# Queries and keys of eight-wide heads: projected dense and spread through DRAM, with two output tiles handled together

## The chip, the cores and the metric

The kernel runs on one core of one Trainium2 chip. The metric is the device time of one execution in microseconds, lower is better. A profiled execution also gives a span, from the first to the last instruction that the profile shows. The engines are PE (TensorE, matrix multiplication), DVE (VectorE), ACT (ScalarE), POOL (GpSimd) and SP (SyncE, which here issues every DMA). PEld is the loading of PE's stationary operand. Each engine takes its own instructions in the order in which they stand, and semaphores tie the engines together.

## The reference, cut to what matters

A model of four blocks works on x of 8 sequences x 256 tokens x 128 features. Each block adds a gated cross attention to a context of the same shape, and then a gated ffn. All of it is float32.

```
x += tanh(g_xattn[0]) * performer(layernorm(x), ctx)       # 16 heads of 8, 32 random features
x += tanh(g_ffn[0])   * (attn0(h) + moe0(h))               # h = layernorm(x); attn0: 16 heads of 8
x += tanh(g_xattn[1]) * topk_attn(layernorm(x), ctx)       # 8 heads of 64, best 64 of 256 keys
x += tanh(g_ffn[1])   * moe1(layernorm(x))
x += tanh(g_xattn[2]) * attn2(layernorm(x), ctx)           # 16 heads of 8
x += tanh(g_ffn[2])   * moe2(layernorm(x))                 # 8 experts and a shared one, 512 wide
x += tanh(g_xattn[3]) * topk_attn3(layernorm(x), ctx)      # 16 heads of 8, best 32 of 256 keys
x += tanh(g_ffn[3])   * moe_attn(layernorm(x))             # 16 experts
```

What the change touches is the attention with 16 heads of 8, in the ffn of block 0 and in the cross attentions of blocks 2 and 3:

```
q = (x @ Wq + bq) / sqrt(8);  k = ctx @ Wk + bk;  v = ctx @ Wv + bv      # split into 16 heads of 8
w = softmax(q @ k.T)            # block 3: over the best 32 keys of each row
out = (w @ v) @ Wo + bo         # block 0's ffn: no Wo, k and v from x itself
```

## The kernel before

The tokens stand in four groups of 512 (two sequences of 256 each), with x in the tiles `xs[g]` of [128 tokens, 4, 128]. Two streams of work are woven together by generators (`side_by_side`). One, `largest_scores`, runs the two top-k attentions: block 1's over all groups, then block 3's over all groups. The other, `others`, runs the rest in a list written out by hand: x0 (the performer), f0 (block 0's ffn), f1, x2, f2 and f3 for each of the four groups. A group of the first stream starts only when the second has finished what comes before it, and the other way round (`may_start`, `started`, `middle`, `largest_1`, `largest_3`). `T_START` holds the times by which the weaving paces the first stream. The generators give the order in which instructions are recorded; a scheduler with a timeline model of its own then sets the order on each engine.

A matmul over heads of 8 reads queries and keys as rows of 32 in the partitions: PE works on four strips of 32 rows at once, so each head has a strip in which eight rows are its data and the rest are zero. Row 8 carries a one in the keys (added by way of the bias, from the column `aug`), and the negated row maximum in the queries, so the shift of the softmax comes out of the same matmul. A tile of queries (`qT`, or `qTk` in block 3) is [128, 4, 256]: four chunks of four heads, for the 256 tokens of one sequence. To get it, `pad_heads` (L231) spreads the weights to 512 columns with zeros between the heads, and `heads_T` (L292) makes four matmuls of 128x256 (L299), one for each chunk, and four ACT passes that add the bias and scale (L305). Block 1's heads of 64 go through `heads_T` too, without a bias (L301).

`attention_T` serves block 0's ffn and block 2. Its `ready` makes the operands of one sequence, computes the scores once for the row maxima (`sm`, L687) and adds the maxima to the queries (L709); `weigh` computes the transposed scores (`sw`, L723), takes the exponential (L737) and multiplies by the values (L357). `attention_largest` serves blocks 1 and 3: `fetch` computes scores (`sp`, L420) into one of several rooms, block 3's selection takes the best 32 by MAX8 and MATCH_REPLACE8 on DVE (L385, L389), POOL makes the mask (L392), and PE adds it to the transposed scores (L574, L584). `prepare` of a sequence runs ahead where the first stream's sequence is known.

`heads_back` (L336) turns the products back to token rows, one tile of 128 tokens at a time: four transposes (L341), a reciprocal (L345) and a product (L347) into `o_sb`. Then it calls `done` for this tile: `out_proj` (L320) transposes (L324), copies (L326), multiplies by Wo (L330) and the bias row (L333), and `add_gated` (L288, L290) adds the result to x.

Every load goes through one helper, `load` (L123), on SP's queue; so all DMAs have line 124. Tiles come from pools with a fixed number of buffers: `work` has four of [128, 1024], `bank` four of PSUM and `qT`, `kT`, `qTk`, `kTk` two each. The three `we2` buffers hold the expert weights of block 2's ffn, which SP loads as buffers come free. `load_context` (L1318) loads and transposes the weights of blocks 2 and 3 through `work` tiles; block 3's `wq` and `wk` use the space of block 1's `wq1` and `wo1`.

At the start, POOL makes constants, multiplies the random features into a block-diagonal weight (L911) once sixteen small DMAs of the features (`rf`) have landed, spreads block 0's weights, and reduces a maximum over the partitions (L894) that the first exponentials of the keys wait for.

After the program that is timed stands a second, exact one, which runs only if a count of wrongly chosen keys is not zero.

Of the kernel before, what the change touches and what calls it, by code (L numbers as in the profile page):

```python
# [90 lines left out]
def gated_blocks_kernel(ctx: ExitStack, tc: tile.TileContext, a, out):  # L91
# [7 lines left out]
    psum = ctx.enter_context(tc.tile_pool(name="psum", bufs=2, space=PSUM))  # L99

    def program(exact):
# [21 lines left out]
        def load(dst, src):  # L123
            nc.sync.dma_start(out=dst, in_=src)
# [106 lines left out]
        def pad_heads(t, w):  # L231

            t = t.rearrange("p (h d) -> p h d", d=32)
            nc.gpsimd.memset(t, 0.0)
            nc.gpsimd.tensor_copy(t[:, :, 0:8], w.rearrange("p (h d) -> p h d", d=8))

        def padded_bias(src, name, scale=1.0):

            t = wt([P, 4], name)
            nc.gpsimd.memset(t, 0.0)  # L240
            for r in range(4):
                load(t[32 * r : 32 * r + 8, :], src.rearrange("(c r d) -> r d c", r=4, d=8)[r])
            if scale != 1.0:
                nc.vector.tensor_scalar_mul(t, t, scale)
            return t

# [41 lines left out]
        def add_gated(g, t, src, gate):  # L288

            nc.vector.scalar_tensor_tensor(xs[g][:, t, :], src, gate, xs[g][:, t, :], ALU.mult, ALU.add)  # L290
# [16 lines left out]

        def values16(w, srcT, width, tag):
# [11 lines left out]
        def out_proj(g, t, o_sb, chunks, w, bias, gate):  # L320

            pt = bank("pt_o")
            for c in range(chunks):
                nc.tensor.transpose(pt[:, c * P : (c + 1) * P], o_sb[:, c * P : (c + 1) * P], ident)  # L324
            oT = out2("oT")
            nc.scalar.copy(oT[:, 0 : chunks * P], pt[:, 0 : chunks * P])  # L326
            yield
            po = bank("po")
            for c in range(chunks):
                nc.tensor.matmul(  # L330
                    po[:, 0:D], lhsT=oT[:, c * P : (c + 1) * P], rhs=w[:, c, :], start=(c == 0), stop=False
                )
            nc.tensor.matmul(po[:, 0:D], lhsT=bias, rhs=biases, start=False, stop=True)  # L333
            add_gated(g, t, po[:, 0:D], gate)

        def heads_back(g, bb, oTs, done):  # L336

            for qc in range(2):
                pn = bank("pn").rearrange("p (c r d) -> p c r d", c=4, r=4)
                for c in range(4):  # L340
# [5 lines left out]
                o_sb = out2("o_sb")[:, 0:D].rearrange("p (c r d) -> p c r d", c=4, r=4)  # L346
                nc.vector.tensor_tensor(  # L347
                    o_sb, pn[:, :, :, 0:8], rec.unsqueeze(3).to_broadcast([P, 4, 4, 8]), ALU.mult
                )
                yield  # L350
                yield from done(g, 2 * bb + qc, o_sb.rearrange("p c r d -> p (c r d)"))
# [699 lines left out]
        wq0, wk0 = w0[:, 1024:1536], w0[:, 1536:2048]  # L1051
# [9 lines left out]
        pad_heads(wq0, st[:, 0:128])  # L1061
        pad_heads(wk0, st[:, 128:256])
        nc.gpsimd.tensor_copy(wv0, st[:, 256:384])
        bq0 = padded_bias(bqkv0[0:128], "bq0", INV_SQRT8)
        bk0 = padded_bias(bqkv0[128:256], "bk0")
        nc.vector.tensor_tensor(bk0, bk0, aug.to_broadcast([P, 4]), ALU.add)
# [12 lines left out]
        class block0_ffn:  # L1079
            def __init__(self, g):  # L1080
                def done(g, t, o):
                    add_gated(g, t, o, tgf[:, 0:1])
                    yield

                self.g, self.att = g, attention_T(g, self.operands, done)
# [19 lines left out]
            def operands(self, bb):  # L1105
                xnT = self.xnT[:, bb * S : (bb + 1) * S]
                qT = heads_T(wq0, xnT, bq0, INV_SQRT8, "qT")
                yield
                kT = heads_T(wk0, xnT, bk0, 1.0, "kT")
# [208 lines left out]
        def load_context(n, tq, tk):  # L1318
            pre = f"L{n}_xattn"
            wq = wt([P, 512], f"wq{n}", tq)  # L1320
            pad_heads(wq, transposed(a[f"{pre}_Wq"]))
            wk = wt([P, 512], f"wk{n}", tk)
            pad_heads(wk, transposed(a[f"{pre}_Wk"]))
# [564 lines left out]
```

## Time and profile before

| | |
|---|---|
| time, three runs | 2543.44, 2546.03, 2556.37 us; median 2546.03 |
| profiled execution: its time, its span | 2546.42 us, 2544.7 us |
| busy | PE 83%, DVE 69%, ACT 45%, POOL 35% of the span |
| mean granted clock of PE | 0.862 |
| DMA | 32.97 MB, 13 GB/s in the mean; from DRAM 29.53 MB read, 1.05 MB written |
| instructions in the profile | 35734 |

How to read it: busy time says how much of the span an engine worked, not how near it is to its limit. "The chain that ended last" is followed back from the last instruction, at each step to what released it; its shares say where a shorter step would have moved the end, until another chain takes over. A group's row gives the line, the engine, the operation, its tiles and shapes, the count, the busy time of the group and the mean of one in ns, and then how long the engine was idle just before and what ended that. A float32 matmul of this kernel leaves two matmul records, so a count on PE is twice the number of instructions. In the table of stages each column is an engine's busy time in that stretch, followed by the granted clock, the share of the DMA engines' time and the rate.

### The profile page before, as it was taken

Reading aid. Unit: us, or ns where it says so; the run is one execution under the profiler, and the core shown is the slowest. Engines: PE = TensorE matmul, PEld = TensorE weight load, DVE = VectorE, ACT = ScalarE, POOL = GpSimd, SP = SyncE. Lnnn points to the kernel's source line nnn. Section 1 sums busy time; section 2 is a strip of 40 time slices with the busy share of each in tenths; the row PEclk is TensorE's granted clock in tenths of the full one; section 3 lists DMA queues with packets and bytes.
Section 4 is the critical chain, followed back from the end, with each engine's and each line's share of the span. In section 5 each row is a group of like instructions: output and inputs, shape, how many; then the busy total and the mean of one; then the engine's idle time right before and its main releaser. Section 6 shows DMA issues by size and latency. Waiting matters only on the chain.

```text
span 2544.7 us, 35734 instructions
## 1 busy us (share of the span) xinstructions
PE 2123.7 (83%) x12068; PEld 1292.4 (51%) x12094; DVE 1762.5 (69%) x5463; ACT 1149.0 (45%) x2437; POOL 879.8 (35%) x2252
## 2 busy tenths in 40 slices
PE   7998888887878778888989868899676975988898
PEld 5655455554445444445444435445343444666677
DVE  4635757756765667665899879894798869798332
ACT  2236556546554677864355433464333542322101
POOL 3104434434432464531334324341233334233000
PEclk8999889978988889998599966899775986999999
DMA  2000001000000000010001100021000110000000
GB/s 63 6 1 2 1 1 32 1 1 1 1 1 1 1 26 1 26 34 22 1 1 42 34 1 1 1 59 50 1 1 1 42 42 1 1 5 1 5 5 6
DMA packets 47896, 32.97 MB, mean 13 GB/s; under 512 B 4747, under 2 KB 42838, under 8 KB 47702
## 3 DMA queue, kind: packets, MB, share of 16 engines
q1 hardware_dynamic: 47702, 30.58, 4.2%
q8 instruction: 97, 1.59, 0.3%
q14 instruction: 97, 0.79, 0.1%
HBM read 29.53 MB, written 1.05 MB: 12 GB/s over the span
## 4 chain that ended last, share of the span: by engine, by line
DVE 39%; PE 36%; ACT 13%; POOL 8%; issue 4%; DMA 0%; DVEq 0%; SPq 0%; ACTq 0%; POOLq 0%
DVE m L385 13%; DVE wk L389 12%; ACT signs L495 4%; PE sm L687 3%; PE sw L723 3%; PE ph L1476 3%; PE pp L299 3%; PE y L1445 2%; DVE nmz L695 2%; PE po L1635 2%; ACT sign L495 2%; PE oT L357 2%; PE o L1216 2%; DVE xe L851 2%; DVE list L542 1%
## 5 line engine op out<-in xcount | busy, mean ns | idle before, releaser
L392 POOL TENSOR_SCALAR mask<-rooms,m 128x256 bf16<-128x256 f32 x192 | 223.3, 1163 | 385.5 <-DVE m L385 353.4
L385 DVE MAX8 m<-wk 128x8 f32<-128x256 f32 x768 | 326.8, 426 | 37.0 <-DVE wk L389 0.9
L723 PE MATMUL sw<-qT,kT 32*128 32x256 f32 x1024 | 172.4, 476 | 68.3 <-ACT eK L599 24.1
L695 DVE TENSOR_REDUCE nmz<-sm 128x4 f32<-128x1024 f32 x128 | 154.9, 1219 | 105.1 <-PE sm L687 96.6
L389 DVE MATCH_REPLACE8 wk<-m,wk 128x256 f32<-128x256 f32 x512 | 208.9, 408 | 0.0
L495 ACT ACTIVATE signs<-room,nt 128x256 bf16<-128x256 f32 x288 | 145.9, 507 | 128.7 <-POOL nt L527 78.5
L687 PE MATMUL sm<-kT,qT 32*128 32x256 f32 x1024 | 152.6, 440 | 40.0 <-DVE nmz L695 28.4
L592 ACT ACTIVATE kept<-mask 128x1024 bf16<-128x1024 bf16 x64 | 67.6, 1057 | 227.3 <-POOL mask L392 227.1
L1476 PE MATMUL ph<-xnT,we 128*128 128x512 f32 x288 | 156.2, 638 | 15.5 <-ACT hT L1477 7.4
L723 PEld LDWEIGHTS sw<-qT,kT 32*128 32x128 f32 x1024 | 101.0, 222 | 128.4 <-DVE nmz L695 32.3
L737 ACT ACTIVATE eT<-sw 128x1024 f32<-128x1024 f32 x128 | 129.6, 1019 | 79.9 <-PE sw L723 73.9
L574 PE MATMUL sw<-qTk,kTk 32*128 32x256 f32 (+1 forms) x768 | 120.8, 456 | 53.6 <-DVE qTk L1383 35.2
L1445 PE MATMUL y<-hT,we 128*128 128x512 f32 x288 | 146.0, 620 | 0.6 <-DVE wb_sb L1457 0.6
L687 PEld LDWEIGHTS sm<-kT,qT 32*128 32x128 f32 x1024 | 92.3, 205 | 101.0 <-DVE nmz L695 42.9
L1477 ACT ACTIVATE hT<-ph,b 128x512 f32<-128x512 f32 x144 | 98.4, 686 | 98.8 <-PE ph L1476 94.4
L599 ACT ACTIVATE eK<-sw 128x1024 f32<-128x1024 f32 x96 | 96.6, 1019 | 89.4 <-PE sw L584 88.5
L420 PE MATMUL sp<-kTk,qTk 32*128 32x256 f32 (+1 forms) x768 | 121.1, 448 | 14.8 <-ACT eT L737 6.5
L357 PE MATMUL oT<-eT,va 128*32 128x256 f32 x1024 | 120.6, 449 | 10.2 <-ACT eT L737 9.3
L392 POOL TENSOR_SCALAR mask<-room,m 128x256 bf16<-128x256 f32 x64 | 74.5, 1164 | 155.2 <-DVE m L385 152.8
L574 PEld LDWEIGHTS sw<-qTk,kTk 32*128 32x128 f32 (+1 forms) x768 | 71.5, 212 | 96.1 <-issue 42.4
L420 PEld LDWEIGHTS sp<-kTk,qTk 32*128 32x128 f32 (+1 forms) x768 | 72.5, 209 | 59.5 <-issue 17.0
L387 POOL TENSOR_SCALAR nmk<-m 128x1 f32<-128x1 f32 x256 | 59.5, 232 | 100.7 <-DVE m L385 100.6
(381 smaller groups left out, 4976.2 us busy)
## 6 DMA issues: line engine op xcount, KB each, us to landing
we<-in_L_ffn_exp_w_dram SPq DMA_DIRECT2D x64, 256.0 KB
we<-in_L_ffn_shared_w_dram SPq DMA_DIRECT2D x8, 256.0 KB
x<-in_x_dram SPq DMA_DIRECT2D x4, 256.0 KB
big_ctx<-in_ctx_dram SPq DMA_DIRECT2D x4, 256.0 KB
w1f<-in_L_ffn_fc_w_dram SPq DMA_DIRECT2D x1, 1024.0 KB
w3a<-in_L_ffn_q_proj_dram SPq DMA_DIRECT2D x4, 256.0 KB
w3a<-in_L_ffn_k_proj_dram SPq DMA_DIRECT2D x4, 256.0 KB
w3b<-in_L_ffn_v_proj_dram SPq DMA_DIRECT2D x4, 256.0 KB
```

What stands on the lines that cost most here:

```text
L357: nc.tensor.matmul(o[32 * r : 32 * r + 32, :], lhsT=va[:, n, 4 * c + r, :], rhs=es[r // 2][:, r % 2, n, :], start=(n == 0), stop=(n == 1),)
L385: nc.vector.max(m8, src[:, j, :])
L389: nc.vector.match_replace(wk[:, j, :], m8, src[:, j, :], LOWEST)
L392: nc.gpsimd.tensor_scalar(mask[:, j, :], s[:, j, :], m8[:, 7:8], 1.0, ALU.is_lt, ALU.mult)
L420: nc.tensor.matmul(sps[r // 2][:, r % 2, qc, :], lhsT=qT[rs, c, qc * P : (qc + 1) * P], rhs=kT[rs, c, :], start=(qc == 0), stop=(qc == 1),)
L495: nc.scalar.activation(to, s[:, j, :], AF.Sign, bias=nt[:, j : j + 1], accum_out=acc[:, j : j + 1])
L574: nc.tensor.matmul(sps[r // 2][:, r % 2, m, :], lhsT=kT[rs, c, m * P : (m + 1) * P], rhs=qT[rs, c, :], start=(m == 0), stop=False,)
L687: nc.tensor.matmul(sps[r // 2][:, r % 2, j, :], lhsT=qT[rs, 2 * cp + j, qc * P : (qc + 1) * P], rhs=kT[rs, 2 * cp + j, :], start=(j == 0), ...
L695: nc.vector.tensor_reduce(nmz[:, qc, 2 * cp : 2 * cp + 2, 2 * h : 2 * h + 2, 8].rearrange("p c r -> p r c"), sps[h], AX.X, ALU.max, negate ...
L723: nc.tensor.matmul(sps[r // 2][:, r % 2, n, :], lhsT=kT[rs, c, n * P : (n + 1) * P], rhs=qT[rs, c, :], start=(n == 0), stop=(n == 1),)
L1445: nc.tensor.matmul(y, lhsT=w2[:, c, :], rhs=hs[c // 2][:, js], start=(c == 0), stop=(c == 3))
L1476: nc.tensor.matmul(pp[:, js], lhsT=w1[:, c * P : (c + 1) * P], rhs=xnT, start=True, stop=True)
```

## The change

Weights of heads of 8 are no longer padded to 512 columns. Their 128 columns are put in another order: strip r of 32 holds rows (d, c) of the four heads 4c + r. One matmul of 128x256 and one ACT pass with bias and scale then make a dense tile of [128, 256]. Four DMAs write its strips to a tile in DRAM of [128, 4, 256], each to the eight rows of a strip that hold data, and a fifth loads the whole tile of 512 KB into `qT` or `kT`. The DRAM tile was filled once, at the start, by a blank of zeros, and for keys with the ones in row 8, so only the eight rows of each strip change later. There are four such DRAM tiles, one for each of `qT`, `kT`, `qTk` and `kTk`, with one buffer.

The bias is brought into the new order by a matmul with a reordered identity, through a `work` tile, and is now one column. Adding `aug` to it is gone. Block 3's weights have their own space.

`heads_back` now writes both tiles of a sequence into one `o_sb` and calls `done` once; `out_proj` transposes both, copies them in one pass and adds both to x in one instruction. Block 0's ffn adds both tiles of a sequence in one instruction too. Block 1 keeps `heads_T` and its own output.

```diff
+    dram = ctx.enter_context(tc.tile_pool(name="dram", bufs=1, space=bass.MemoryType.DRAM))
...
-        def pad_heads(t, w):
-
-            t = t.rearrange("p (h d) -> p h d", d=32)
-            nc.gpsimd.memset(t, 0.0)
-            nc.gpsimd.tensor_copy(t[:, :, 0:8], w.rearrange("p (h d) -> p h d", d=8))
-
-        def padded_bias(src, name, scale=1.0):
-
-            t = wt([P, 4], name)
-            nc.gpsimd.memset(t, 0.0)
+        def heads_in_rows(t, w):
+
+            t = t.rearrange("p (r d c) -> p r d c", r=4, d=8)
+            w = w.rearrange("p (c r d) -> p r d c", c=4, r=4)
             for r in range(4):
-                load(t[32 * r : 32 * r + 8, :], src.rearrange("(c r d) -> r d c", r=4, d=8)[r])
-            if scale != 1.0:
-                nc.vector.tensor_scalar_mul(t, t, scale)
+                nc.gpsimd.tensor_copy(t[:, r], w[:, r])
+
+        def heads_bias(src, name, scale=1.0):
+
+            st = work("st")
+            heads_in_rows(st[:, 0:P], ident)
+            load(st[:, P : P + 1], src.unsqueeze(1))
+            pb = bank("pb")
+            nc.tensor.matmul(pb[:, 0:1], lhsT=st[:, 0:P], rhs=st[:, P : P + 1], start=True, stop=True)
+            t = wt([P, 1], name)
+            nc.vector.tensor_scalar_mul(t, pb[:, 0:1], scale)
             return t
...
+        spread_heads = {}
+        blank = work("blank").rearrange("p (c q) -> p c q", c=4)
+        for ones, tags in ((0, ("qT", "qTk")), (1, ("kT", "kTk"))):
+            if ones:
+                nc.gpsimd.tensor_copy(blank, aug.unsqueeze(2).to_broadcast([P, 4, S]))
+            else:
+                nc.gpsimd.memset(blank, 0.0)
+            for tag in tags:
+                spread_heads[tag] = dram.tile([P, 4, S], F32, tag="d_" + tag, name="d_" + tag)
+                load(spread_heads[tag], blank)
...
-            nc.vector.scalar_tensor_tensor(xs[g][:, t, :], src, gate, xs[g][:, t, :], ALU.mult, ALU.add)
+            x = xs[g][:, 2 * t : 2 * t + 2, :] if len(src.shape) == 3 else xs[g][:, t, :]
+            nc.vector.scalar_tensor_tensor(x, src, gate, x, ALU.mult, ALU.add)
...
+        def padded_heads_T(w, src, bias, scale, tag):
+
+            pp = bank("pp")[:, 0:S]
+            nc.tensor.matmul(pp, lhsT=w, rhs=src, start=True, stop=True)
+            dense = act.tile([P, S], F32, tag="dense", name="dense", bufs=2)
+            nc.scalar.activation(dense, pp, AF.Identity, bias=bias, scale=scale)
+            to = spread_heads[tag]
+            for r in range(4):
+                load(to[32 * r : 32 * r + 8].rearrange("d c q -> (d c) q"), dense[32 * r : 32 * r + 32, :])
+            dst = act.tile([P, 4, S], F32, tag=tag, name=tag, bufs=2)
+            load(dst, to)
+            return dst
...
-        def out_proj(g, t, o_sb, chunks, w, bias, gate):
+        def out_proj(g, bb, o_sb, w, gate, bias):
 
             pt = bank("pt_o")
-            for c in range(chunks):
-                nc.tensor.transpose(pt[:, c * P : (c + 1) * P], o_sb[:, c * P : (c + 1) * P], ident)
-            oT = out2("oT")
-            nc.scalar.copy(oT[:, 0 : chunks * P], pt[:, 0 : chunks * P])
+            for qc in range(2):
+                nc.tensor.transpose(pt[:, qc * P : (qc + 1) * P], o_sb[:, qc * P : (qc + 1) * P], ident)
+            oT = out2("oT")[:, 0:S]
+            nc.scalar.copy(oT, pt[:, 0:S])
             yield
-            po = bank("po")
-            for c in range(chunks):
-                nc.tensor.matmul(
-                    po[:, 0:D], lhsT=oT[:, c * P : (c + 1) * P], rhs=w[:, c, :], start=(c == 0), stop=False
-                )
-            nc.tensor.matmul(po[:, 0:D], lhsT=bias, rhs=biases, start=False, stop=True)
-            add_gated(g, t, po[:, 0:D], gate)
+            po = bank("po")[:, 0:S].rearrange("p (t d) -> p t d", t=2)
+            for qc in range(2):
+                nc.tensor.matmul(po[:, qc, :], lhsT=oT[:, qc * P : (qc + 1) * P], rhs=w, start=True, stop=False)
+                nc.tensor.matmul(po[:, qc, :], lhsT=bias, rhs=biases, start=False, stop=True)
+            add_gated(g, bb, po, gate)
...
-                yield from done(g, 2 * bb + qc, o_sb.rearrange("p c r d -> p (c r d)"))
+            yield
+            yield from done(g, bb, o_sb)
...
-                kT = heads_T(wk, cT, bk, 1.0, "kT" + k)
+                kT = padded_heads_T(wk, cT, bk, 1.0, "kT" + k)
                 yield
-                qT = heads_T(wq, xnT, bq, INV_SQRT8, "qT" + k)
+                qT = padded_heads_T(wq, xnT, bq, INV_SQRT8, "qT" + k)
```

## The prediction, made before the changed kernel was run

> **What bounds the kernel now.** I read the page first (engines, chain), then the table of stages, then the groups of the lines that the change touches, then the chain around them, piece by piece.
>
> ```profile
> span 2544.7 us, 35734 instructions
> ...
> PE 2123.7 (83%) x12068; PEld 1292.4 (51%) x12094; DVE 1762.5 (69%) x5463; ACT 1149.0 (45%) x2437; POOL 879.8 (35%) x2252
> ...
> DVE 39%; PE 36%; ACT 13%; POOL 8%; issue 4%; DMA 0%; DVEq 0%; SPq 0%; ACTq 0%; POOLq 0%
> ```
>
> No single engine sets the time: the chain that ends last is on DVE and PE about equally, and on DMA not at all. The table of stages says where which one rules:
>
> ```profile
> core 0: us, PE busy (x) PEld busy (x) DVE busy (x) ACT busy (x) POOL busy (x), PEclk, DMA share, GB/s
> ...
> 100.00:1160.00 1060.00, 893.78 (x5510) 523.42 (x5522) 680.08 (x2003) 619.28 (x1562) 430.09 (x1533) 0.89 0.03 9
> 1160.00:2160.00 1000.00, 815.47 (x4035) 444.62 (x4046) 815.83 (x2708) 424.73 (x661) 356.02 (x526) 0.80 0.06 18
> ```
>
> From 100 to 1160 us PE is the busiest (84%); from 1160 to 2160 us DVE is as busy, with the top-k search of block 3 (L385, L389). All projections that change lie between 100 and 2170 us. In the second stretch the chain leaves DVE only where a new group's queries and keys are made; there it runs through the very lines that change (eight matmul records are four matmuls, so one takes 0.43 us at full clock):
>
> ```profile
> 1161.23 1.92 PE pp L299 x8
> ...
> 1163.59 1.73 PE pp L299 x8
> ...
> 1178.56 2.22 PE pp L299 x6
> ...
> 1184.03 2.36 PE pp L299 x10
> ```
>
> ```profile
> 2061.96 2.99 PE pp L299 x8
> ...
> 2066.34 1.99 PE pp L299 x8
> ...
> 2068.99 1.09 PE sp L420 x16
> ```
>
> **The change part by part.** Base: the profiled execution, 2546.4 us with a span of 2544.7; the median of the runs, 2546.0, is the same within 0.4.
>
> *Projections, removed.* 48 calls (block 0's ffn, blocks 2 and 3; 4 groups, 2 batches, queries and keys) each drop from four matmuls and four biased ACT passes to one and one: 144 of each.
>
> ```profile
> L299 PE MATMUL pp<-xnT,wq 128*128 128x256 f32 x192 | 52.7, 411 | 4.1 <-DVE qTk L1383 1.4 <-ACT kT L305 1.1 <-ACT xnT L284 1.1
> ...
> L305 ACT ACTIVATE kT<-pp,bk 128x256 f32<-128x256 f32 x64 | 26.5, 469 | 8.1 <-PE pp L299 7.5 <-PE sw L723 0.4
> ```
>
> PE loses 144 x 0.43 = 62 us, ACT 144 x 0.47 = 68 us. Only what the chain holds counts: L299 is 2.6% of it, 66 us; going through its pieces, about 55 of them are calls that change, the rest block 1's. I put 5 of the 55 (2062 to 2068 us, group 3) aside, as its path is counted whole below. Three quarters of 50 is 37 us. L305 on the chain sums to 8 us, so 5 for ACT. A shortened chain meets the next one; before 1160 us and in the handovers PE stands back to back on the chain, so I take 0.8: **-34 us** (bounds -15 at 0.35, -42 at 1).
>
> *The round trip, added.* Per call four stores of 32 KB and one load of 512 KB, all on SP's queue: 240 DMAs. The trace has no such trip; the nearest rows are the one DMA that the chain waits for, a 64 KB load, and the rate of the big weight loads:
>
> ```profile
> 92.48 0.33 SPq L124
> ...
> 92.98 1.83 DMA st<-in_L_xattn_Wo_dram
> ```
>
> ```profile
> 405.00:412.50 7.50, 5.41 (x44) 3.48 (x41) 6.49 (x19) 5.42 (x20) 3.65 (x14) 0.77 0.94 265
> ```
>
> Issue to use of a small one is 0.33 + 1.83 = 2.2 us, issues follow every 0.43 us (sixteen in 6.88 us at the start). Fourth store issued 1.3 after the dense tile and landed by 3.3 to 3.5; the load 2.2 plus 448 KB at 265 GB/s (1.7), landed 7.2; with matmul and ACT 8 us from projection to use. In a pair, the second call's stores share SP with the first: 11 us. Bounds: 6 and 9 if writes land faster or loads share engines, 11 and 14 if both legs take half again.
>
> Against that stands the PE work that the built program's order puts between a projection and its first reader (L687 or L420), each instruction at its group's mean busy time. In the other calls it is 8.1 to 57 us, which hides the trip. It is short in these: block 0, group 0, second batch, a pair, 8.4 us (needs 11: 2.6 missing); x2 of group 1, second batch, a pair, 6.9 (4.1); x3 of group 0, 7.4 for queries (0.6); x2 of groups 2 and 3, second batch, 5.8 (2.2 each); x3 of groups 1 and 2, first batch, 5.0 (3.0 each); x3 of group 3: before, 7.0 us from the first projection (2061.96) to L420 (2068.99), now 11 (4.0). DVE and ACT wait behind the same readers there, so all of it is on the path: **+22 us** (bounds +5 with the short trip, +53 with the long one, where the calls with 8 to 13 us join).
>
> *What a waiting SP holds up.* A load stands at SP's head until its four stores have landed, and the expert weights (for L1476 and L1445) queue behind it, at most 8 us for a pair. They have three buffers and an expert takes over 8 us, so they are due some 16 us later: 0. Were the cover gone, one pair for each of x2(1) to x2(3) would cost up to 5 us.
>
> *PE's clock.* The call at 2062 us took 2.99 us for what took 1.73 at 1163 us: PE had idled and ran at half clock. The trace's row charges nothing more for a place that was cold already. [...] I take **+2**, since work of the other stream breaks most waits.
>
> *Start.* POOL fills a blank tile (a memset of 128x1024 takes 0.95), two DMAs write it out, and the copy that makes the second blank waits for them; ahead of the reduction of L894, a place with no slack:
>
> ```profile
> 17.64 0.31 POOL L1063 COPY w<-st 128x128 f32<-128x128 f32 x1
> 24.58 0.38 POOL L894 PARTITION_ALL_REDUCE k_stab<-k_top  x1 [6.63 <-issue]
> 32.15 0.61 POOL L945 TENSOR_SCALAR qf<-qf 128x512 f32<-128x512 f32 x1 [7.19 <-issue]
> ```
>
> The two writes go out after six of the sixteen rf loads (about 10 us), 1 MB at 265 GB/s lands about 15; the copy takes 1.2, eight identity copies about 1.2, L911 1.07, seven weight copies 1.2: POOL reaches L894 near 20.2 where it did at 17.95, and both later starts follow. **+2.5** (bounds 0, if POOL catches up, and +6).
>
> *Weight setup.* Each bias now takes one of the four `work` buffers, a load, four POOL copies, a matmul and a DVE pass. Block 2's stand where the chain already waits for such a load (92.98): **+3** for two blocks (0 to +6). The four bias DMAs each that go, and the zero fills, were covered.
>
> *Outputs.* 48 updates of x at 344 ns become 24 of 128x256 (480 ns for L869's of that size): DVE -5; 32 ACT copies of 265 ns become 16 of about 375: -2.5. A third is on the chain: **-2**. The projection now waits for both tiles; that is behind the next batch.
>
> Sum: -34 + 22 + 2 + 2.5 + 3 - 2 = **-6.5**, that is 2540.
>
> **The rivals.**
> *A longer trip (slower).* One mechanism: the write to DRAM and the read of it take half again, 11 us alone and 14 in a pair. Then the eight places cost 53 instead of 22: -34 + 53 + 5.5 = +24.5, plus 4 for a cold PE, **2575**. It decides from where the waits exceed the 36 us of savings, a trip of about 9.5 us. For it: no DRAM write is read back anywhere in this trace. Against: small DMAs land after 2.2 us here.
> *The saving is not on the path.* The chain through PE is back to back partly because other PE work was free to move; with 0.35 of the saving, -15 + 22 + 7.5 - 2 = +12.5, **2559**. For it: 0.80 clock and full DVE after 1160 us. Against: the pp pieces stand in the handovers where DVE starves.
> *The trip is hidden (clearly faster).* Elapsed time between projection and reader is longer than PE work alone (PE is 84% busy), so waits cost 8; the saving counts in full and ACT's 68 us also shorten the counting loop of L495 (4.5% of the chain): -42 + 8 + 5.5 - 2 - 5 = -35, **2511**. For it: readers queue behind both streams. Against: the scheduler has filled those gaps already.
> That the change does less than it says is excluded: the built program has 138 PE and 162 ACT instructions fewer and 226 SP instructions more.
>
> **How the numbers follow.** Forecast 0.45 (own range 2526 to 2556, since every order on every engine is made anew: some 15 us), longer trip 0.2, not on the path 0.15, hidden 0.2. 0.5%, about what a measurement of this kernel tells from no change, is 12.7 us: faster is under 2533, slower over 2559. Faster: a third of the forecast and the hidden case, 0.35. Slower: a sixth of the forecast, the longer trip, two thirds of the off-path case: 0.37. Same: 0.28. Range 2503 to 2580.
>
> **What would show it.** Right: L299's changed groups at a quarter of their counts; loads into qT and kT landing about 7 us after the dense tile; waits of PE for those loads only in the eight places named, summing to 15 to 30 us; L894 two to three us later. The first rival: trips over 9.5 us, waits above 36. The second: waits as forecast, yet the stretch from 100 to 1160 us no shorter. The third: waits under 10. The forecast is wrong if waits appear in other places, or if expert weights come late (the matmuls of `ph` waiting for a DMA).

## The result: 1.7% slower, and the profile after

The changed kernel takes 2594.11 us in the median of four runs (2580.8 to 2602.63), the kernel before 2546.39 (2543.44 to 2556.37, four runs on the same chip). The ratio is 1.0169, with a 95% interval of 1.0141 to 1.0197. The forecast was 2540, its range ended at 2580. The profiled execution took 2591.64 us with a span of 2589.9. In what follows a ratio of 0.001 is 2.5 us of the time before, and every ratio is taken against runs of the kernel before on the same chip.

From the page of the changed kernel: engines, the row of the granted clock, the DMA queue, and the chain.

```profile
span 2589.9 us, 35528 instructions
...
PE 2147.0 (83%) x11791; PEld 1283.9 (50%) x11818; DVE 1759.2 (68%) x5439; ACT 1090.2 (42%) x2275; POOL 886.7 (34%) x2284
...
PEclk9988878877887889987688856699565977989899
...
q1 hardware_dynamic: 64310, 64.15, 8.3%
...
PE 37%; DVE 35%; ACT 12%; POOL 7%; issue 5%; DMA 2%; SPq 1%; DVEq 0%; another core or an unknown queue 0%; ACTq 0%; POOLq 0%
```

ACT's busy time fell by 59 us, as it should. PE's did not: it has 138 instructions less (144 matmuls of 0.43 us, 62 us, against a few that the biases add), and was busy 23 us longer (2123.7 before). It was also idle 22 us longer (span less busy time), and the two together are the 45 us by which the span grew. The chain now holds DMA and SP's queue (3% together; before 0%), and PE has not become a smaller part of it. The table of stages of the changed kernel says where PE's time went (columns as in the table of before):

```profile
core 0: us, PE busy (x) PEld busy (x) DVE busy (x) ACT busy (x) POOL busy (x), PEclk, DMA share, GB/s
100.00:1160.00 1060.00, 884.81 (x5328) 505.05 (x5340) 675.55 (x1987) 590.97 (x1489) 427.67 (x1526) 0.85 0.07 21
1160.00:2160.00 1000.00, 819.90 (x3832) 431.40 (x3843) 776.23 (x2553) 389.23 (x562) 341.03 (x515) 0.74 0.12 35
```

The granted clock fell from 0.89 to 0.85 in the first stretch and from 0.80 to 0.74 in the second. Between 1160 and 2160 us PE left 3832 records where it had left 4035. Of these 203, 144 are the matmuls that were taken away (24 calls, three matmuls each, two records a matmul); the other 59 are work that is late. DVE got through 2553 operations instead of 2708. The trace lists the stretches of half clock; summed, they are 704 us before and 930 after. They became longer more than they became many: 59 stretches with a median of 6.8 us before, 69 with 10.2 after. PE's busy time inside them is 521 us before and 732 after. If PE gets through half as much there (the records of a projection follow each other every 216 ns at full clock and every 427 at half), half of the difference, 106 us, is what the lower clock added to PE's busy time. That is an estimate, and it does not close: 106 less the 62 of the missing matmuls would be 44, where 23 were measured.

The trips themselves look as the forecast drew them. This is the chain through a pair of calls, block 2's group 1, second batch (start, duration, what; pieces under 0.15 us are left out):

```profile
1181.61 1.16 PE pp L328 x2
1182.80 0.48 ACT dense L330
1183.30 0.32 SPq L125
1183.67 0.42 SPq L125
1184.13 0.42 SPq L125
1184.60 1.56 DMA d_kT<-dense
1186.23 0.34 SPq L125
1186.61 0.43 SPq L125
1187.08 2.85 DMA d_qT<-dense
1189.99 3.21 DMA qT<-d_qT
...
1193.33 2.09 PE sm L717 x16
```

Four issues take 1.3 us, the last store lands 1.56 us after its issue (2.85 in the second set, which goes out behind the 512 KB load of the first), the load takes 3.21. From the projection to the reader it is 11.7 us here; in the call at 1513 us, alone, 8.0. PE's waits for these loads, in us in total, times, longest:

```profile
PE sp L450 <- DMA qTk<-d_qTk: 9.1, 3, 7.3
PE sm L717 <- DMA qT<-d_qT: 8.0, 2, 5.4
PE sm L717 <- DMA kT<-d_kT: 7.2, 2, 5.0
```

That is 24.3 us in seven waits. (The expectations below speak of 32 us and eight waits; that sum, taken tile by tile, counted one wait of block 3 a second time as an idle of the weight loads. PE alone is 24.3.)

### The profile page after: what moved, and what is told of

Its sections match the earlier page's. It is cut to its first block, busy times and chain, and to the rows that moved or that the text cites. A ratio compares the mean times of both kernels' runs of the same rounds, so it can differ in the third digit from the quotient of the medians.

```text
span 2589.9 us, 35528 instructions
## 1 busy us (share of the span) xinstructions
PE 2147.0 (83%) x11791; PEld 1283.9 (50%) x11818; DVE 1759.2 (68%) x5439; ACT 1090.2 (42%) x2275; POOL 886.7 (34%) x2284
## 3 DMA queue, kind: packets, MB, share of 16 engines
q8 instruction: 95, 1.56, 0.3%
## 4 chain that ended last, share of the span: by engine, by line
PE 37%; DVE 35%; ACT 12%; POOL 7%; issue 5%; DMA 2%; SPq 1%; DVEq 0%; another core or an unknown queue 0%; ACTq 0%; POOLq 0%
DVE m L415 12%; DVE wk L419 11%; ACT signs L525 4%; PE sm L717 4%; PE ph L1505 3%; PE y L1474 3%; PE sw L753 2%; ACT sign L525 2%; PE o L1245 2%; DVE nmz L725 2%; PE po L1664 2%; PE oT L387 2%; DVE xe L881 1%; PE pqk L1609 1%; PE pqk L1610 1%
## 5 line engine op out<-in xcount | busy, mean ns | idle before, releaser
L717 PE MATMUL sm<-kT,qT 32*128 32x256 f32 x1024 | 166.9, 500 | 65.3 <-DVE nmz L725 27.5
L604 PE MATMUL sw<-qTk,kTk 32*128 32x256 f32 (+1 forms) x768 | 142.9, 527 | 43.8 <-DVE qTk L1412 18.9
L717 PEld LDWEIGHTS sm<-kT,qT 32*128 32x128 f32 x1024 | 100.6, 235 | 134.6 <-DVE nmz L725 46.6
L1505 PE MATMUL ph<-xnT,we 128*128 128x512 f32 x288 | 155.6, 636 | 11.8 <-ACT hT L1506 8.4
L450 PE MATMUL sp<-kTk,qTk 32*128 32x256 f32 (+1 forms) x768 | 134.5, 497 | 35.3 <-ACT eT L767 15.0
L604 PEld LDWEIGHTS sw<-qTk,kTk 32*128 32x128 f32 (+1 forms) x768 | 83.2, 248 | 96.6 <-issue 28.6
L450 PEld LDWEIGHTS sp<-kTk,qTk 32*128 32x128 f32 (+1 forms) x768 | 79.6, 233 | 87.6 <-issue 25.8
```

The source lines that it names most:

```text
L450: nc.tensor.matmul(sps[r // 2][:, r % 2, qc, :], lhsT=qT[rs, c, qc * P : (qc + 1) * P], rhs=kT[rs, c, :], start=(qc == 0), stop=(qc == 1),)
L604: nc.tensor.matmul(sps[r // 2][:, r % 2, m, :], lhsT=kT[rs, c, m * P : (m + 1) * P], rhs=qT[rs, c, :], start=(m == 0), stop=False,)
L717: nc.tensor.matmul(sps[r // 2][:, r % 2, j, :], lhsT=qT[rs, 2 * cp + j, qc * P : (qc + 1) * P], rhs=kT[rs, 2 * cp + j, :], start=(j == 0), ...
L1505: nc.tensor.matmul(pp[:, js], lhsT=w1[:, c * P : (c + 1) * P], rhs=xnT, start=True, stop=True)
```

## Experiments

Two kinds of number are read beside each time. "PE waits" are PE's idle us that end with a load of the trip. "Half clock" is the sum of the trace's stretches of half clock. Before: 0 and 704. Changed: 24.3 and 930. Both come from one profiled execution of each kernel. How far they move when the time does not is told by two kernels that take as long as the one before, `outputs_only` and `placebo`: half clock is 740 us in both, and PE is busy for 2151.7 and 2137.1 us (2123.7 before). A smaller difference in either says nothing. The edits are shown in short, with shortened names.

**The change in parts.** `spread_only` is the changed kernel with the outputs of before (the edit in words):

```
-def heads_back, out_proj, add_gated, done: two tiles of one sequence together
+def heads_back, out_proj, add_gated, done: one tile at a time, as before
```

`outputs_only` is the kernel before with the opposite exchange. `saving_only` and `trip_only` are the kernel before with another `heads_T` in the 48 calls:

```
 saving_only
-for c in range(4): matmul(pp[c], lhsT=w[:, c * P : (c + 1) * P], rhs=src); activation(dst[:, c, :], pp[c], ...)
+matmul(pp, lhsT=w[:, 0:P], rhs=src)
+activation(dst, pp.unsqueeze(1).to_broadcast([P, 4, S]), bias=bias[:, 0:1], ...)
```

```
 trip_only
 dst = heads_T(w, src, bias, scale, tag)
+for r in range(4): load(to[32 * r : 32 * r + 8], dst[32 * r : 32 * r + 8])
+load(dst, to)
```

> The changed kernel with the outputs going back tile by tile as before; the dense projections and the trip through DRAM stay. Theory A (the trip: waits for the loads plus a matmul engine that runs longer at half clock) and theory B (the saving in matmuls was never on the path, the waits alone are left): both 2594 give or take 8, since the pairing is worth 2. Theory C (the pairing of outputs does the harm, by making one batch's output wait for two tiles): 2565 or less.

> The kernel before with only the pairing of outputs: padded projections, no trip. Theories A and B: 2544, that is 2 less than before, give or take 8 for the order that the scheduler makes anew. Theory C: 2575 or more.

> The kernel before with each of the 48 projections cut to one matmul and one ACT pass that writes the first quarter of heads to all four places (heads 4 to 15 are left out, heads 0 to 3 stand in for them); no transfer, no wait, no pairing. Removes 144 matmuls (62 us of PE) and most of 68 us of ACT. Theory A: the saving counts as forecast, -34, so 2512. Theory B: it is off the path, 2540 or above.

> The kernel before with all its padded projections, whose rows 0 to 7 of each 32 are stored to DRAM by four DMAs and the whole tile is loaded back over itself before use, as in the change. The trip alone, with nothing saved. Theory A: the waits of some 32 us and as much again or more by the clock, +80, so 2626, with half-clock time rising from 704 us to some 900. Theory B: the waits alone, +45, so 2591, half-clock time up by no more than 60 us. My forecast's own sum had +22 to +29 for it: 2575.

Measured: `spread_only` 1.0178 (1.0127 to 1.0229), `outputs_only` 1.0011 (0.9987 to 1.0036), `trip_only` 1.0292 (1.0244 to 1.0341). So the pairing of outputs neither costs nor brings anything that can be seen, and theory C falls. The trip alone costs 74 us. With the dense projections beside it the loss is 45, so they are worth 29 there (give or take 18).

`saving_only` was a poor choice. Its keys make the count of wrongly chosen keys non-zero, so that the exact second program ran too, and its 5453 us compare with nothing. Within its first program the 29th addition of block 3's maxima to the queries starts at 2300 us. Before it did at 2281, in `outputs_only` on the same chip at 2288 and in the `placebo` below at 2298. So nothing that can be seen was gained by then, with 144 matmuls less and no trip. Its table of stages:

```profile
100.00:1160.00 1060.00, 883.76 (x5274) 503.02 (x5272) 678.17 (x1991) 594.52 (x1479) 425.95 (x1525) 0.84 0.03 7
1160.00:2160.00 1000.00, 794.21 (x3917) 416.29 (x3916) 805.10 (x2666) 420.34 (x600) 353.09 (x523) 0.77 0.07 19
```

The clock is lower than before in both stretches (0.84 and 0.77 for 0.89 and 0.80), though no load is waited for. That is weak evidence: in `outputs_only`, which does all the work of before in the same time, the two are 0.85 and 0.81, so a clock as low as the change's 0.85 in the first stretch need not cost anything.

In `trip_only` PE waits 43.3 us for the trip's loads (its table of waits: us, times, longest):

```profile
PE sp L441 <- DMA qTk<-d_qTk: 24.6, 4, 8.2
PE sm L708 <- DMA qT<-d_qT: 14.4, 3, 7.1
PE sm L708 <- DMA kT<-d_kT: 4.3, 1, 4.3
```

Its half clock is 816 us, between the 764 at most of theory B and the some 900 of theory A; its 74 us lie near A's 80. So the trip costs more than the waits that PE shows for it, but the clock does not follow it as far as A had said. `trip_only` has three matmuls and three ACT passes more ahead of each trip than the changed kernel. So part of what the dense projections are worth beside a trip may be that the trip starts earlier: PE's waits are 19 us shorter in the changed kernel.

**The length of the trip, the clock, the load of PE, the traffic.** `direct` spreads from SBUF to SBUF; `warm_wait` puts matmuls ahead of the places that wait; `three_more` puts the saved matmuls back, unread; `traffic_only` sends the DMAs with nobody waiting.

```
 direct
 dst = act.tile([P, 4, S], F32, tag=tag)
+load(dst, spread_heads[tag])            # only blank rows
 matmul(pp, lhsT=w, rhs=src); activation(dense, pp, ...)
-for r in range(4): load(to[32 * r : 32 * r + 8], dense[32 * r : 32 * r + 32])
-load(dst, to)
+for r in range(4): load(dst[32 * r : 32 * r + 8], dense[32 * r : 32 * r + 32])
```

```
 warm_wait, behind the second projection of eight calls
+for _ in range(16): matmul(junk, lhsT=ident, rhs=ident)
```

```
 three_more
 matmul(pp, lhsT=w, rhs=src)
+for _ in range(3): matmul(other_half_of_bank, lhsT=w, rhs=src)
```

```
 traffic_only, on the kernel before
 dst = heads_T(w, src, bias, scale, tag)
+for r in range(4): load(to[32 * r : 32 * r + 8], dst[32 * r : 32 * r + 8])
+load(unread_in_dram, to)
```

> The changed kernel, but the dense tile is spread from SBUF straight to the rows of its destination by the same four DMAs; the load of the whole tile from DRAM goes ahead of the matmul and brings only the blank rows. Same number and size of DMAs, one leg (about 3.2 us) less between projection and reader. Theory A (exposed waits of the trip, and the clock that they cost): 8 places lose 3.2 us each, 26, and some 20 of slowed matmuls, so 45 less than the change, about the time of before. Theory B (the waits alone, no clock): 26 less than the change. Theory C (not the length of the trip but the traffic and a full SP queue): no more than 8 less.

> The changed kernel with 16 unread matmuls of 128x128 (about 4 us in all) put behind the second projection in eight calls that precede the waits: block 0's second batch of group 0, block 2's second batches of groups 1 to 3, block 3's first batches. 128 matmuls, about 32 us of PE at full clock. Theory A in the form that the idle PE of these eight waits halves the clock: half-clock time falls from 930 to below 830 us and the time by 20 or more. If the clock falls for another reason (PE's load in general, after 144 matmuls were taken away): half-clock time within 50 us of 930, and the time 0 to 25 longer.

> The changed kernel with three more matmuls of the same size, unread, behind each of the 48 dense projections: PE's work is that of before again, ACT's saving and the trip stay. If the lighter load of PE is what let the clock fall: half-clock time back to some 800 us, and the time within 8 of the change. If the clock falls through the waits: half-clock time unchanged within 50 us, and the 62 us of matmuls cost 30 to 50, towards the time of the trip alone (1.029 of before).

> The kernel before with the change's DMAs beside it and nobody waiting for them: the padded tiles are stored to DRAM by four DMAs a call, and the whole tile goes from there to an unread place in DRAM; the projections' readers take the tile as ACT left it. Blanks are written at the start as in the change. Theories A and B (waits of the readers): 0 to +8 (the start alone, +2.5). Theory C (traffic, SP's queue holding the expert weights): +30 or more.

`direct`: 0.9999 (0.9980 to 1.0018), that is 43 us less than the change (give or take 9) with the same number and size of DMAs. PE's waits that are left, from its table of waits:

```profile
PE sm L716 <- DMA qT<-dense: 2.7, 2, 1.4
PE sp L449 <- DMA qTk<-dense: 2.1, 1, 2.1
PE sm L716 <- DMA kT<-dense: 1.0, 1, 1.0
```

5.8 us for 24.3. So 18.5 us of waits went and 43 us of time. PE's busy time fell by 19 us with the same instructions, and it spent less of it at half clock (677 us for 732). Theory A's 45 is what came; the waits alone would have given 26 by theory B, 18.5 by the corrected count. The traffic alone cannot be the cause of the loss, as it is still all there. What `direct` shows is that the second leg is what costs; how the 24 us beyond the waits come about it does not show, and its order of instructions is made anew as well.

`warm_wait`: 1.0125 (1.0099 to 1.0150), 11 us less than the change (give or take 10), although PE has 128 matmuls more. Half clock fell to 818 us, just below the 830 that was named, PE waits to 11.8 (the added matmuls fill part of them); the time fell by less than the 20 named. `three_more`: 1.0196 (1.0176 to 1.0216). 144 matmuls of 0.43 us, 62 us of work, cost 7 us (give or take 9). Its table of cores has the span and the mean granted clock:

```profile
core 0: 2602.5 us, clock 0.847
```

The changed kernel has 0.821, and it is not this execution alone: the four runs have 0.845 to 0.847, those of the changed kernel 0.819 to 0.826. Half clock fell from 930 to 797 us. PE's busy time rose by 12 us for 62 us of work. The waits even rose to 33.2, for in most calls ACT's dense pass starts only 0.04 us after the last of the four matmuls, so the trips start later too. So the clock fell in the change also because PE's load fell, not through the waits alone.

`traffic_only`: 1.0094 (1.0065 to 1.0123), 24 us, where both A and B had said 8 at most and C 30 or more. Nobody waits for a load of the trip in it.

**What is not the trip.** Three edits of the kernel before, and one of `direct`:

```
start_only    + the four blanks in DRAM and the two fills of `blank`, nothing else
stores_only   traffic_only without load(an unread DRAM tile, to)
placebo       + spare = cst([P, 4], "spare"); nc.gpsimd.memset(spare, 0.0)
direct_lean   two blanks, read only; nc.vector fills two tiles, in place of nc.gpsimd filling one twice
```

> The kernel before with only the two blanks and their four writes to DRAM at the start; nobody uses them. The built program has the order of the kernel with traffic and no waits on PE, DVE, ACT and POOL, instruction for instruction, but 240 DMAs less. That kernel took 1.009 of before. If its 24 us are the DMAs (engines shared with the weights, SP's queue): here 1.001, my start term of 2.5 us. If they are the start and the order that the scheduler makes anew: here 1.009 as well.

> The kernel with traffic and no waits, without the 48 transfers of 512 KB from DRAM to DRAM; the 192 stores of 32 KB stay. Again the same order on the four engines. If the 512 KB transfers cost: 1.001 to 1.004, below the 1.009 with them. If the order and the start cost: 1.009. If the stores hold SP's queue and the tiles: 1.009 with start_only near 1.001.

> The kernel before with one unread 128x4 memset more on POOL at the start. Its work is the same; the scheduler moves 13 of 8511 PE instructions and 143 of 4376 DVE ones against before. What it differs by is what an order made anew is worth: within 0.2% if orders this near to each other cost nothing, up to 0.5% either way if the time hangs on them.

> The one-leg spread from SBUF to SBUF with two blanks instead of four in DRAM (they are only read now), both filled by DVE from tiles of their own, so that POOL waits for nothing at the start. If the start is part of what is left of the loss: 5 to 10 us less than the one-leg spread, 0.997 of before or below, and faster than both kernels. If not: within 0.3% of 1.000.

`start_only` takes 1.0057 (1.0033 to 1.0080), `stores_only` 1.0077 (1.0052 to 1.0103), `placebo` 0.9992 (0.9981 to 1.0003), `direct_lean` 1.0004 (0.9970 to 1.0039). So of the 24 us of `traffic_only` some 14 are there with no DMA but those of the start. The start is late by only some 2 us in these kernels (block 0's first addition of maxima begins at 136.5 to 137.4 us, before at 134.9). By elimination some 12 of the 14 are put down to the order that the scheduler makes anew: of the records in the trace it moved 330 of 12067 on PE and 555 of 5463 on DVE against before, in `traffic_only` and `stores_only` the same number. The placebo's order, much nearer to that of before (18 and 192), costs nothing. No run has this order without the blanks, so that it is the order is not shown. What remains for the 240 DMAs themselves is 9 us with overlapping intervals, not settled apart from none. A leaner start brings nothing.

**Which step of the sum.** `three_legs` copies the stored pieces once more, from DRAM to DRAM, before the load. `padded_where_late` keeps the padded projections in block 3's first batches. `direct_three` is `direct` with the matmuls of `three_more`. `act_more` puts ACT's passes back, not the matmuls.

```
 three_legs
 for r in range(4): load(to[32 * r : 32 * r + 8], dense[32 * r : 32 * r + 32])
-load(dst, to)
+for r in range(4): load(further[32 * r : 32 * r + 8], to[32 * r : 32 * r + 8])
+load(dst, further)
```

```
 padded_where_late
-kT = padded_heads_T(wk, cT, bk, ...); qT = padded_heads_T(wq, xnT, bq, ...)
+project = heads_T if n == 3 and bb == 0 else padded_heads_T     # with padded weights and biases for heads_T
+kT = project(wk, cT, bk, ...); qT = project(wq, xnT, bq, ...)
```

```
 act_more
 activation(dense, pp, AF.Identity, bias=bias, scale=scale)
+for _ in range(3): activation(other_half_of_bank, pp, AF.Identity, bias=bias, scale=scale)
```

> The changed kernel with one leg more in each trip: the four stored pieces of 32 KB are copied from DRAM to a second DRAM tile before the load. One leg gave 1.000 of before, two legs 1.017. Theory A (the length of the trip, exposed in the eight places and paid twice, by the wait and by the slower matmuls behind it): a third leg of about 3 us costs 24 in the eight places, some 10 in six more whose cover of 8 to 13 us it exceeds, and the clock: 1.031 to 1.040. Waits alone: 1.025 to 1.031. If the length of the trip is not what costs: up to 1.022.

> The changed kernel, but block 3's first batches of each group (8 of 48 calls, four of the eight places, with 16.8 of the 32 us in which PE stood idle for a load of the trip) keep the padded projections of before, with no trip; the other 40 calls are dense and go through DRAM. Theory A: 17 of waits, up to 10 of clock, less 6 for the matmuls and passes that come back: 1.008 to 1.011. If the cost is spread over all 48 trips: one sixth of the 43 us, 7, so 1.014.

> The one-leg spread with three unread matmuls behind each of the 48 dense projections, so that PE's work is that of before. There nobody waits long for a load. If the saved matmuls are worth what I forecast (0.8 of 37): 1.011. If PE gives the saving back through the clock, as in the two-leg kernel, where the same matmuls cost 7: within 1.004, with half-clock time below 820 us where the one-leg spread had 865.

> The changed kernel with three more ACT passes of 128x256 behind each dense one, unread, into the spare half of the bank: ACT's 144 passes, 68 us, are back, behind the pass that the trip starts from. If ACT's saving is what paid in the dense projections: 1.024 or above. If the saving was worth the 5 that I counted for it, or paid by a shorter way to the trip's start: 1.015 to 1.020.

`three_legs`: 1.0290 (1.0239 to 1.0341). The time does grow with the trip, by 31 us (give or take 15), at the low end; "waits alone" had 1.025 to 1.031. PE's waits rose by 44 us, to 68.2. So a longer wait is not paid twice everywhere: here 0.7 us of time came with each us of wait, in the step from two legs to one it was 2.3. Theory A's 1.031 to 1.040 was missed. `padded_where_late`: 1.0103 (1.0069 to 1.0138), as theory A had it. Eight of 48 calls carry 17 us of the loss (give or take 11), with 16.4 us of waits gone. So over a third of the cost sits in a sixth of the calls, those whose readers come soon.

`direct_three`: 1.0047 (1.0025 to 1.0068), 12 us more than `direct` (give or take 7), between the two numbers that were named. Half clock falls from 865 to 729 us. In the profiled executions PE's busy time rises by 27 us for the 62 us of work, and its idle time falls by 22: a part of the work went into time in which PE had stood idle. `act_more`: 1.0247 (1.0208 to 1.0285), 20 us more than the change (give or take 12), half clock 1012 us. So ACT's passes are not hidden, as I had taken them to be. They also hold the bank of the projection longer; that is not separated.

**The setup of the biases.** ACT stands still once in the changed kernel for a bias, since its `work` buffer is one of those that the exponentials use (the table of waits of the changed kernel):

```profile
ACT L767 <- DMA st<-in_L_xattn_bq_dram: 6.3, 1, 6.3
```

`bias_by_dma` (the change) and `direct_lean_bias` (`direct_lean`) bring the biases without it:

```
 def heads_bias(src, name, scale=1.0):
-  st = work("st"); heads_in_rows(st[:, 0:P], ident); load(st[:, P:P+1], ...); matmul(pb, ...); ...
+  t = wt([P, 1], name)
+  for c in range(4):
+    load(t[c::4, :], src[32*c : 32*c+32].unsqueeze(1))
   ...
```

> The changed kernel with each of its six dense biases put in the order of the rows by four DMAs of 128 bytes straight into its own tile, in place of the load into a work buffer, the four POOL copies of the identity and the matmul. In the changed kernel ACT waits 6.3 us for such a load at the start of block 3. If that wait is on the path, as its chain has it: 6 to 8 us less than the change, 1.014. If the weights' own loads take its place: 1.017.

> The one-leg spread with two blanks, with the biases brought by DMA as well. It takes away the two costs that the runs have sized: the second leg (43 us) and the bias load that ACT waits for (6). If they add up: 0.997 of before, from 0.994 to 0.999, faster than both kernels. If the order made anew outweighs it: 1.000 to 1.005.

`bias_by_dma` takes 1.0170 (1.0141 to 1.0199): the wait of 6.3 us is gone, and nothing is gained. What is late next is the trip: the chain then runs through a weight load of block 3 into the same pair of calls, and PE's waits for `qT` rise from 8.0 to 12.3 us. `direct_lean_bias`: 1.0032 (1.0016 to 1.0047), slower than before. No version that I ran is clearly faster than the kernel before.

## Why the prediction was wrong, step by step

The forecast was a sum of -6.5 us; measured are +43 by the ratio. By the same steps:

| step | forecast | what the runs show |
|---|---|---|
| projections, PE's part | -30 | back in place they cost 7 (change) and 12 (one leg) |
| projections, ACT's part | -4 | back in place they cost 20 |
| round trip | +22 | PE waits 24.3 us; alone it costs 74 with 43.3 of waits, and its second leg 43 with 18.5 |
| what a waiting SP holds up | 0 | no wait of PE for expert weights; all the DMAs at most 9, unsettled |
| PE's clock | +2 | by elimination some 24 behind the trip, and 18 to 23 of the PE part above; not shown apart |
| start | +2.5 | 2 |
| weight setup | +3 | a wait of 6.3, worth nothing |
| outputs | -2 | +3 (-3 to +9) |
| order made anew | in the range, 15 either way | some +12 in one kernel (by elimination), 0 in another |

Two steps failed. The trip was priced at the waits of PE that it causes, with 2 us more for the clock; the runs show that it costs more than them, 74 us alone where 43.3 are waits, 43 for the second leg where 18.5 are. And the saving of 34 us was counted as kept; put back, PE's 62 us of matmuls cost 7 and 12.

*Round trip.* Its length was right (8.0 us alone and 11.7 in a pair for 8 and 11), and so was the sum of the waits, 24.3 for 22. The sum owes something to luck. The places were mostly right: block 0's group 0 with 5.0 (2.6 forecast), block 2's group 1 with 5.4 (4.1) and group 3 with 2.6 (2.2), block 3's group 0 with 1.6 (0.6) and group 3 with 7.3 (4.0). These five took 21.9 us where 13.5 were forecast. Block 2's group 2 and block 3's groups 1 and 2 were hidden or nearly so (0.2 for the 8.2 forecast), and one of 2.2 in block 0 was not forecast. So the waits had come almost where and as long as the prediction had named for being right, and the time was wrong all the same: its signs looked at waits and at the start alone, and none at PE's clock or at what the saving brings.

*PE's clock* is where the terms that failed seem to meet. The +2 was my estimate, with the reason that "work of the other stream breaks most waits". No run shows this term, nor the 4 for a cold PE in the first rival; what the runs show in their place is a granted clock of 0.819 to 0.826 in the change, where the kernel before has 0.862 in its profiled execution, and half clock of 930 us for 704. I took the clock for a toll at each wait. In these runs it does not follow the waits alone. First the trip: with one leg less, 18.5 us of waits go and 43 us of time, so some 24 hang on more than PE's waits, and PE's busy time at half clock falls by 55 us. Second the saving itself: 62 us of matmuls put back cost 7 and 12 us, with 133 and 136 us less at half clock. Of what PE had been relieved of, it lost a large part by working slower (its busy time rose by 12 and 27 us for the 62).

That the clock is the cause of the 24 us is argued and not shown. `three_legs`, where waits rose by more than the time did, speaks against a fixed price for each wait. `three_more` has 0.847 for 0.821 and 62 us of matmuls more, and is no faster; `direct` has 0.831 to 0.840 and takes as long as before at 0.858, and PE's busy time alone moves by 28 us between kernels of equal time. An order of instructions that is worse or better by the size of `start_only` would be half of the 24. What the 24 us are stays open.

*Projections.* The term of -34 rested on PE's share of the chain, taken at 0.8. The chain's pieces were measured at the clock of before, and the clock did not stay. The chain was also misread. From 100 to 1160 us PE is 33% of it, not back to back, and ACT 26%, DVE 21%, POOL 17%; that ACT's passes put back cost 20 us fits this. From 1160 to 2160 us the chain leaves DVE not only for a new group's queries and keys: PE has 289 us of it, of which L299 is 35 and the expert matmuls L1476 and L1445 are 114. The second rival counted 0.35 of the saving, 13 of the 37 us on PE, as on the path. The 7 and 12 measured are near that, and in `direct_three` a part of the work did fill idle time; it had not foreseen the clock, and it had the round trip too cheap like the forecast. Beside the trip the dense projections are worth 29 in all (`trip_only` less `spread_only`, give or take 18), near the 34 by luck: the parts that were tried one by one are ACT's passes and the shorter waits, not PE's matmuls. Without a long trip, in `direct`, nothing is left of it: my own terms would make that kernel some 25 us faster than before, and it is the same.

*Start* was right: the reduction that was at 24.6 us is at 26.5 in the changed kernel, 2.0 later. Its instruction, with count, shortest, median and longest ns, first and last start:

```profile
L924 POOL PARTITION_ALL_REDUCE k_stab<-k_top x1: 378/378/378, 26.5 to 26.5; - x1
```

*Order.* I put the order made anew into the range and not into the sum. `start_only` hints at its size, some 12 us with hardly any work added. Its sign in the changed kernel is not known, since no run has the change with the order of before.

The first rival, a trip half as long again, fell: the trip is as long as I said. It gave the best number, 2575, for a reason that did not hold.

## What to carry to other kernels

A matmul taken away was not worth its duration here, 7 and 12 us of 62: look at how much of the chain is PE's in that stage and at its granted clock, and ask whether what stays will hold the clock (0.819 to 0.826 in the change, 0.845 to 0.847 with the 144 matmuls put back). A DMA round trip had a large part of its price in the few places where its reader comes soon (eight of 48 calls held 17 of the 43 us), so cost it place by place, and try one leg before two. And where a scheduler makes the order anew, compare with an edit that changes the order and hardly any work, before a half per cent is put down to a mechanism.

## What was not expected of the hardware

PE can be busy all the time and stay at half clock. In the kernel before, for 33 us (its table of stages, one stretch):

```profile
1233.00:1266.00 33.00, 32.78 (x147) 17.56 (x150) 23.48 (x81) 12.95 (x19) 9.73 (x15) 0.51 0.00 1
```

PE is busy 32.78 of 33 us, and the granted clock is 0.51. The chain goes through this stretch on PE; these are its pieces for a part of it:

```profile
1243.91 2.01 PE sw L723 x8
1245.91 0.99 PE oT L357 x2
1246.91 1.05 PE pn L341 x4
1247.95 0.55 PE pt_r L827 x4
1248.51 1.00 PE oK L357 x4
1249.51 2.01 PE sw L723 x8
```

Most of it is attention matmuls whose stationary operand has 32 rows or 32 columns: 106 of the stretch's 147 records on PE are of the forms 32*128 and 128*32 (L357, L723, L574, L420). The stretch also holds transposes (L341, L827). Over the whole execution before, 38% of the time of L357 and 39% of that of L723 fall into half clock, but 10% and 6% of that of the expert matmuls L1476 and L1445, which are 128*128 in the trace. The two sides are not clean: of the projections L299, 128*128 as well, 23% fall into half clock, of the matmuls L964, 32*128, 15%, and of the transposes L341, 128*128, 40%. In the changed kernel the longest stretch of half clock is 78 us, and PE was busy 62.42 of 76 us inside it (its table of stages):

```profile
1496.00:1572.00 76.00, 62.42 (x294) 36.02 (x294) 52.50 (x154) 20.68 (x28) 19.61 (x31) 0.50 0.06 18
```

The prediction met half clock where PE had stood idle (for 4.6 us before the call at 2062 us); here PE was at half clock for 33 us of work with 0.2 us idle. What ends such a stretch is not shown. In `three_more`, 144 matmuls of 128*128 more went with 133 us less of half clock. But neither the width of the operands nor the transposes sort the lines above, since L299 and L964 fit neither, and no run here varies the width alone.

Executions of one and the same kernel differ along the same line: over 77 executions of the kernel before on four chips, from 2542.56 us at a clock of 0.866 to 2571.5 at 0.849, the time falls by 15 us for each 0.01 of the mean granted clock, with a correlation of -0.93. Which of the two leads is not shown by that.
